# Two graph layers on one core: w of pairs 2 to 27 turned by VectorE and DRAM, filter taps in two row groups, conv results written pair by pair

## The chip, the core and the metric

The kernel runs on 1 core of one Trainium2 chip, in float32 throughout. The metric is the device time of one execution in microseconds (us). PE is TensorE, DVE VectorE, ACT ScalarE, POOL GpSimd and SP SyncE, whose queue issues nearly all DMAs.

## What is computed

There are 64 graphs of 256 nodes with 256 channels, x of shape (64, 256, 256), and a 0/1 adjacency of shape (64, 256, 256). Layer 0, then layer 1:

```python
xc = transpose(x)                                   # channels first
h = relu(bn1(conv1x1(xc)))
x_conv = transpose(relu(bn2(conv17(h, pad=8)) + xc))
s = x @ w_se.T + b_se                               # 3 numbers per node
A = exp(-dist(s)) * adj
x_nmp = A @ relu(x @ w_msg.T + b_msg)
gi = concat(x_conv, x_nmp) @ w_ih.T + b_ih          # r, z, n
gh = x @ w_hh.T + b_hh
r = sigmoid(gi_r + gh_r); z = sigmoid(gi_z + gh_z)
n = tanh(gi_n + r * gh_n)
x = layernorm(x + (1 - z) * n + z * x)
h = layernorm(x)                                    # layer 1
conv = (adj @ h) @ W_rel + b_rel + h @ W_root
x = layernorm(x + x + relu(conv))
```

## The kernel before, in words

**Pairs and blocks.** Graphs go in 32 pairs (`pair(p)`), and the 17-tap convolution in 8 blocks of 8 graphs, four pairs each (`conv1(b)`, then `conv(b)`). The convolution is done by splitting the signal: DVE folds a block (L771) and splits it in a tree of additions and multiplications (L593 to L612 and L679), PE multiplies each leaf by its filter matrix (`product`, L707, tiles ps_k), DVE takes the products out of PSUM (L725 and L726; in block 0 L745) and merges them (L623 to L647), and the last steps (L901 to L905) give the result in slots V0 of X. `kept` (L911) then scales it by the second batch norm and writes it to XC, in slices over the time index j that cover all 8 graphs.

**Filters.** `filters()` makes the leaf matrices once. The 17 taps of 7 output channels are laid side by side by POOL (L542, tile ws), turned by PE (L548, tile tT; ACT evicts, L550), and multiplied by the tap matrix (119 rows, 329 columns; L565, tile ps_w; ACT evicts into W2, L568). There are 74 such blocks of 7 channels, four to a round. The matrices stay in W2 for block 0, and `store_w2` writes them to DRAM; later blocks load them back three at a time into cs (L700).

**One pair.** From xT (x with channels on the partitions) PE makes messages (ps_msg, L1092), distances (ps_sT, ps_dist), and with exp and the mask AT; then ps_nmp (L1139). xc is the conv result plus xT, relu'd (L1145, L1146). The gates (L1179) multiply three sources, xT, nmp and xc, by the gate weights WB: pairs 0, 1 and 31 (`PLAIN`) in 8 plain products (tiles ps_g), the others in 14 products after Strassen's scheme (ps_a, ps_b, ps_d). The tail of the gates (L1246 to L1255) leaves w, which is four times the value to be normed, in wT with channels on the partitions. `norm` turns it back: 8 PE transposes per pair into ps_wT (L1276); ACT copies them to x1 and sums each row (L1285), squares (L1291), and POOL makes the mean and the power -1/2 in q (L1289 to L1300). `project` multiplies wT by both layer-1 matrices (ps_hy, L1311), and DVE scales by q into HY (L1313). `aggregate` multiplies by the adjacency (ps_agg, L1325), adds, norms once more, and stores (L1355). HY, x1 and wT exist once, so a pair waits for the one before to be done with them. Pairs 28 to 31 (`late`) take their statistics on DVE from ps_wT.

**x.** `conv1(b)` fetches x for two graphs (L799 from block 3 on: 16 DMAs of 32 KB in runs of 128 B, so that one DVE operation in 32x32 blocks, L813, finishes the transpose), multiplies (L847), writes relu'd results to DRAM (hd), from where `conv` loads them (L861).

**Order.** Nothing runs as written. Each operation is recorded with a key (`prog.at`, `spread`), and `scheduled` orders each engine's queue by simulated durations and keys; pair p's key is `due = FIRST_GATES + p * PERIOD`, and its steps lie at set distances from it. The order is then fixed: an engine, SP among them, waits at its next instruction. PSUM has 8 banks, with shares: gates 4, conv 3, the rest 6.

Of the kernel before, what the change touches and what calls it, by code (L numbers as in the profile page):

```python
# [54 lines left out]
OB = 7  # L55
HQ = 2 * M * C * (M + 1)
XC_SLOTS = BG + 2
FIRST_GATES, PERIOD, GATE_TIME = 143.0, 60.5, 17.0
AHEAD_FROM, AHEAD_TO, W_DEEP = -20.0, 10.0, 2
CONV1_FROM, CONV1_TO, CONV_FROM, CONV_OUT, CONV_TO = -10.0, 120.0, -6.0, -70.0, -30.0  # L60
PAIR_LEAD, FILTER_LEAD, LOAD_AHEAD = 20.0, 15.0, 12.0
SMALL_RUNS, TURN_FROM = 2.5, 3
# [192 lines left out]
def dram_cells(ap):  # L255

    name = ap.tensor.name
    if not name.startswith(("w2m", "xt", "hd")):
        return []
    dims = list(ap.ap)  # L260
    top = ap.offset + sum(s * (n - 1) for s, n in dims)
    return [(name, u) for u in range(ap.offset // DRAM_UNIT, top // DRAM_UNIT + 1)]


class Engine:
# [4 lines left out]
    def __getattr__(self, method):  # L270
        program, name = self.program, self.name

        def call(*args, hold=(), need=(), lines_up=0, **named):
            line = sys._getframe(1 + lines_up).f_lineno
            outs = [v for v in (named.get("out"), named.get("accum_out"), named.get("out_")) if v is not None]
            outs += [] if "out" in named else [args[0]]
            ins = [v for v in list(args) + list(named.values()) if not any(v is o for o in outs)]
            if method == "matmul" and not named.get("start", True):
                ins.append(outs[0])

            def places(vs):
                return [v if isinstance(v, View) else dram_cells(v) for v in vs
                        if isinstance(v, View) or hasattr(v, "tensor")]
            n = max((v.size() for v in outs if isinstance(v, View)), default=0)
            moved = 0
            if method == "dma_start":
                v = outs[0] if isinstance(outs[0], View) else named["in_"]
                dur, moved = 0.06, v.size() * v.at.shape[0] * 4
                if program.joined is not None:
                    moved *= SMALL_RUNS  # L290
            elif name == "tensor":
                turned = method == "transpose" or named.get("is_transpose")
                dur = 0.109 if turned else 2 * max(0.109, n * 0.8333e-3 + 0.0025)
            elif name == "vector":
                dur = 0.182 if method == "bn_aggr" else 0.147 + 1.044e-3 * (args[1].size() if method == "bn_stats" else n)
                dur += 0.06 * (method == "scalar_tensor_tensor" and isinstance(args[2], View))
            elif name == "scalar":
                dur = 0.16 + 0.83e-3 * n + 0.11 * sum(isinstance(named.get(k), View) for k in ("bias", "scale"))
                dur += 0.2 * ("accum_out" in named)
                where = outs[0].at[0].ravel()  # L300
                dur += 0.9e-3 * n * (n > 1 and "accum_out" not in named and where[1] - where[0] > 1)
            else:
                dur = 1.5 if ALU.pow in args else 0.45 + 1.5e-3 * n
            program.add(name, method, args, named, line, places(ins) + list(need), places(outs) + list(hold), dur, moved)
        return call
# [104 lines left out]
def gnn_two_layers(  # L410
# [66 lines left out]
    xt_dram = tc.dram_tile([B // 2, P, C, 2 * N], F32, name="xt")  # L477
    W2 = sb("w2all", [P, C, NM, D], "first")
    taps = sb("taps", [TAPS * OB, NM * OB], "filters")

# [3 lines left out]
    tb = np.einsum("kf,op->kofp", tap_matrix(), np.eye(OB, dtype=np.float32)).reshape(TAPS * OB, NM * OB)  # L484
# [30 lines left out]
    def filters():  # L515
        pieces, groups = [], []
        for c in range(C):
            for o0, o1 in ((0, 12 * OB), (12 * OB, 24 * OB), (24 * OB, D)):
                starts = [min(o, D - OB) for o in range(o0, o1, OB)]
                for a in range(0, len(starts), 4):  # L520
                    groups.append((len(pieces), starts[a:a + 4]))
                pieces.append((c, o0, o1))
        WT, TT = {}, {}
        WS, AHEAD = {}, 4
        wts = ring("wt", [P, TAPS, D - 24 * OB], 2, "filters")
        wss = ring("ws", [P, 4, TAPS, OB], AHEAD, "filters")
        tTs = ring("tT", [TAPS * OB, 4, P], 2, "filters")
# [8 lines left out]
        def laid(i):  # L536
            piece, starts = groups[i]
            n, o = len(starts), starts[0] - pieces[piece][1]
            if i == 0 or groups[i - 1][0] != piece:
                fetch(piece + 1)  # L540
            WS[i] = next(wss)
            G.tensor_copy(WS[i][:, :n], WT[piece][:, :, o:o + n * OB].rearrange("p k (b o) -> p b k o", o=OB))  # L542

        def turned(i):
            ps, n = bank("ps_tT"), len(groups[i][1])
            with prog.group():
                for k in range(n):
                    PE.transpose(ps[:TAPS * OB, k * P:(k + 1) * P], WS[i][:, k].rearrange("p k o -> p (k o)"), ident)  # L548
            tT = next(tTs)
            A.copy(tT[:, :n].rearrange("k b p -> k (b p)"), ps[:TAPS * OB, :n * P])  # L550
            return tT
# [5 lines left out]
        for i, (piece, starts) in enumerate(groups):  # L557
            c = pieces[piece][0]
            if i + AHEAD < len(groups):
                laid(i + AHEAD)  # L560
            if i + 1 < len(groups):
                TT[i + 1] = turned(i + 1)
            for a, o in enumerate(starts):
                ps = bank("ps_w")
                PE.matmul(ps[:, :NM * OB], TT[i][:, a, :], taps, start=True, stop=True)  # L565
                skip = OB - D % OB if o == D - OB else 0
                pv = ps[:, :NM * OB].rearrange("p (f o) -> p f o", o=OB)
                A.copy(W2[:, c, :, o + skip:o + OB], pv[:, :, skip:])  # L568

# [203 lines left out]
    def graphs_of(b):  # L773
        left, g = BG, 0
        while left:
            slot = (b * BG + g) % XC_SLOTS
            n = min(left, XC_SLOTS - slot)
            yield g, n, slot
            g, left = g + n, left - n

# [3 lines left out]
    def conv1(b):  # L784
# [5 lines left out]
        def fetch(g):  # L790
            if b >= TURN_FROM:
                XN[g] = xn_ahead[:, :4 * D]
                blocks = XN[g].rearrange("p (c g b i) -> p g c b i", c=C, g=2, i=SQ)
                with prog.group():
                    for a in range(P // SQ):
                        for k in range(2):
                            for c in range(C):
                                at = c * P + a * SQ
                                SP.dma_start(out=blocks[a * SQ:(a + 1) * SQ, k, c], in_=x[b * BG + g + k][  # L799
                                    :, at:at + SQ].rearrange("(b j) i -> j b i", j=SQ))  # L800
# [57 lines left out]
    def conv(b):  # L858
# [48 lines left out]
        def kept(js):  # L907
            for o in range(C):
                v = X[:, V0:V0 + M].rearrange("p j (c e) -> p j c e", c=C)[:, js, o, :]
                for g, n, slot in graphs_of(b):  # L910
                    A.activation(XC[:, o, slot:slot + n].rearrange("p g (t j) -> p j g t", j=M)[:, js],  # L911
                                 v[:, :, g * M:(g + n) * M].rearrange("p j (g t) -> p j g t", t=M), AF.Identity,
                                 bias=bn_shift[1][:, o:o + 1], scale=bn_scale[1][:, o:o + 1])

        if b == 0:
            for q in range(4):
                second(q)
                third(q)
                third(q + 4)
                kept(slice(q, M, 4))  # L920
            return
        for j in range(4):
            second(j)
        yield "out"
        for j in range(4):
            third(j)
            third(j + 4)
            kept(slice(j, M, 4))
# [12 lines left out]
    spread(at2, at3, 12.0, 70.0)  # L941
# [47 lines left out]
    prog.at(58.0, 0.01)  # L989
# [8 lines left out]
    nmp = nmps[:, 1:5].rearrange("p (c g) n -> p c g n", c=C)  # L998

# [17 lines left out]
    run(first)  # L1017
    at6 = len(prog.ops)
    spread(at4, at6, 33.0, FIRST_GATES - 4)
    conv1(1)  # L1020
# [20 lines left out]
    for c in range(C):  # L1041
        V.tensor_scalar(beta[:, c, :], ones, gb[:, 1, c:c + 1], None, ALU.mult)
# [26 lines left out]
    def pair(p):  # L1069
# [98 lines left out]

        def product(ps, i, second, start):
# [33 lines left out]
        if plain:  # L1203
            prog.at(due, 2 * GATE_TIME / 44)
            for gs in ((0,), (1,)) if apart else ((0, 1),):
                for T in (RG, ZN):
                    for f in range(C):
                        for g in gs:
                            a = bank("ps_g", "gate")
                            for k in range(C):  # L1210
                                product(a, (f, k, g), T is ZN, k == 0)
# [52 lines left out]
        def norm(gs):  # L1264
# [5 lines left out]
            for g in gs:  # L1270
# [34 lines left out]
        def project(gs, q):  # L1305
            prog.at(due + 2 * GATE_TIME + 8, 0.6)
# [8 lines left out]
        def aggregate(gs):  # L1315
            prog.at(due + 2 * GATE_TIME + 16, 0.4)
# [47 lines left out]
    for b in range(NB):  # L1364
# [11 lines left out]
        if b + 1 < NB:  # L1376
# [6 lines left out]
            run(coming)  # L1383
            at3 = len(prog.ops)
            spread(at1, at2, start + CONV_FROM, start + span + CONV_OUT)
            spread(at2, at3, start + span + CONV_OUT, start + span + CONV_TO)
            if b + 2 < NB:
# [85 lines left out]
```

## Time and profile before

| | |
|---|---|
| Median of 3 runs (lowest, highest) | 2065.92 us (2064.77, 2066.36) |
| The profiled execution, its span | 2065.45 us, 2063.7 us |
| Mean granted PE clock | 0.995 |
| Busy: PE, DVE, ACT, POOL | 2029.6, 1678.4, 1047.5, 296.9 us |
| PE idle: hrow waiting for L1042; nmp for L1132; ps_wT for L1255 | 6.3, 6.2, 3.4 us |
| DMA | 241.21 MB in 284683 packets, 110469 of them under 512 B |
| L1276 on PE, L813 on DVE, L799 on SP | x256 (busy 33.7 us), x20 (1239 ns), x320 (median 449 ns) |
| PE: L548 and L565; ACT: L550 and L568 | 10.9 and 43.7 us; 11.0 and 33.2 us |

The span runs from the first to the last instruction; the execution's own time is 1.75 us longer. A group line has the line of the code, the engine, the operation, out<-in, shapes and count, then busy time and the mean of one in ns. Matmul durations overlap[...]. A window line has the stretch, its length, busy time (and instructions) of PE, weight loads, DVE, ACT and POOL, the granted clock, the mean busy share of 16 DMA engines, and GB/s. A timeline line has start, duration, engine, line, operation, tiles and count; brackets hold idle time ahead of it and what ended it.

### The profile page before, as it was taken

Reading aid. Unit: us, or ns where it says so; the run is one execution under the profiler, and the core shown is the slowest. Engines: PE = TensorE matmul, PEld = TensorE weight load, DVE = VectorE, ACT = ScalarE, POOL = GpSimd, SP = SyncE. Lnnn points to the kernel's source line nnn. Section 1 sums busy time; section 2 is a strip of 40 time slices with the busy share of each in tenths; the row PEclk is TensorE's granted clock in tenths of the full one; section 3 lists DMA queues with packets and bytes.
Section 4 is the critical chain, followed back from the end, with each engine's and each line's share of the span. In section 5 each row is a group of like instructions: output and inputs, shape, how many; then the busy total and the mean of one; then the engine's idle time right before and its main releaser. Section 6 shows DMA issues by size and latency. Waiting matters only on the chain.

```text
span 2063.7 us, 28744 instructions
## 1 busy us (share of the span) xinstructions
PE 2029.6 (98%) x10332; PEld 1645.4 (80%) x10332; DVE 1678.4 (81%) x2587; ACT 1047.5 (51%) x2460; POOL 296.9 (14%) x520
## 2 busy tenths in 40 slices
PE   9989999999999999999999999999999999999997
PEld 6868779778887788877887778877888778887875
DVE  7983798899968998889968998799887899875644
ACT  7453534754446544565447544475445554465432
POOL 4010210111111111101101121112110111111100
PEclk9999999999999999999999999999999999999999
DMA  8834363334433264334532354333452224211100
GB/s 213 265 99 156 105 205 121 105 120 146 152 97 113 78 184 138 95 100 125 176 98 97 101 155 149 104 116 84 151 159 80 72 77 153 93 38 61 41 21 31
DMA packets 284683, 241.21 MB, mean 117 GB/s; under 512 B 110469, under 2 KB 269180, under 8 KB 284540
## 3 DMA queue, kind: packets, MB, share of 16 engines
q1 hardware_dynamic: 283998, 238.94, 37.8%
q8 instruction: 82, 1.34, 0.3%
q14 instruction: 61, 0.50, 0.1%
q10 hardware_dynamic: 542, 0.43, 0.1%
HBM read 177.85 MB, written 61.47 MB: 116 GB/s over the span
## 4 chain that ended last, share of the span: by engine, by line
PE 92%; DVE 5%; ACT 1%; issue 1%; POOL 0%; POOLq 0%; DVEq 0%; ACTq 0%
PE ps_a L1179 21%; PE ps_k L707 15%; PE ps_hy L1311 10%; PE ps_d L1179 10%; PE ps_msg L1092 5%; PE ps_agg L1325 5%; PE ps_b L1179 5%; PE ps_nmp L1139 5%; PE ps_c L847 5%; PE ps_g L1179 4%; PE ps_w L565 2%; PE ps_wT L1276 1%; DVE XF L679 1%; PE ps_dist L1125 1%; PE ps_tT L548 0%
## 5 line engine op out<-in xcount | busy, mean ns | idle before, releaser
L707 PEld LDWEIGHTS ps_k<-XF,cs 128*128 128x128 f32 x2632 | 316.3, 192 | 15.6 <-issue 9.6
L707 PE MATMUL ps_k<-XF,cs 128*128 128x128 f32 x2632 | 318.3, 275 | 0.0
L1311 PE MATMUL ps_hy<-wrr,wT 128*128 128x512 f32 x512 | 228.3, 593 | 1.5 <-ACT XF L724 1.5
L1179 PE MATMUL ps_a<-nmp,WB 128*128 128x256 f32 x696 | 207.5, 380 | 0.0
L1311 PEld LDWEIGHTS ps_hy<-wrr,wT 128*128 128x128 f32 x512 | 95.4, 190 | 103.0 <-issue 92.1
L1191 ACT COPY ZN<-ps_a 128x512 f32<-128x512 f32 x116 | 68.0, 586 | 194.1 <-PE ps_a L1179 193.8
L1179 PE MATMUL ps_a<-tx,WB 128*128 128x256 f32 x522 | 158.2, 385 | 0.2
L1193 ACT ACTIVATE RG<-ps_a,bhh 128x512 f32<-128x512 f32 x116 | 79.2, 683 | 139.9 <-PE ps_a L1179 107.2
L1179 PEld LDWEIGHTS ps_a<-nmp,WB 128*128 128x128 f32 x696 | 132.5, 190 | 18.3 <-ACT nmp L1141 0.2
L1335 ACT ACTIVATE HY<-HY 128x256 f32<-128x256 f32 x112 | 45.7, 408 | 177.9 <-DVE HY L1329 172.4
L1092 PE MATMUL ps_msg<-wms,xT 128*128 128x260 f32 x512 | 133.4, 383 | 0.0
L679 DVE TENSOR_TENSOR XF<-XF 128x512 f32<-128x512 f32 (+3 forms) x128 | 126.3, 1009 | 5.3 <-ACT XF L760 3.3
L1139 PE MATMUL ps_nmp<-AT,msg 128*128 128x256 f32 x512 | 120.6, 384 | 6.4 <-DVE AT L1132 6.2
L1313 DVE SCALAR_TENSOR_TENSOR HY<-ps_hy,q,hrow 128x512 f32<-128x512 f32 x128 | 95.4, 747 | 36.1 <-PE ps_hy L1311 31.8
L1325 PE MATMUL ps_agg<-HY,adja 128*128 128x256 f32 x512 | 120.1, 380 | 2.6 <-DVE HY L1313 2.6
L1325 PEld LDWEIGHTS ps_agg<-HY,adja 128*128 128x128 f32 x512 | 96.1, 190 | 29.5 <-issue 12.9
L1139 PEld LDWEIGHTS ps_nmp<-AT,msg 128*128 128x128 f32 x512 | 96.3, 192 | 21.9 <-DVE AT L1132 6.6
L1179 PEld LDWEIGHTS ps_a<-tx,WB 128*128 128x128 f32 x522 | 94.4, 191 | 21.2 <-issue 6.9
L847 PE MATMUL ps_c<-xTc,w 128*128 128x512 f32 x232 | 107.5, 594 | 1.4 <-ACT xTc L827 1.4
L1092 PEld LDWEIGHTS ps_msg<-wms,xT 128*128 128x128 f32 x512 | 93.4, 190 | 14.2 <-issue 1.8
L1179 PE MATMUL ps_a<-xc,WB 128*128 128x256 f32 x348 | 103.6, 379 | 0.8 <-ACT xc L1146 0.8
L1289 POOL TENSOR_SCALAR total<-total 128x4 f32<-128x4 f32 x28 | 13.5, 484 | 631.4 <-ACT x L1285 631.4
(205 smaller groups left out, 4519.7 us busy)
## 6 DMA issues: line engine op xcount, KB each, us to landing
cs<-w2m SPq DMA_DIRECT2D x105, 768.0 KB, 4.9
adjm<-in_adjT_dram SPq DMA_DIRECT2D x64, 256.0 KB, 2.8
xT<-xt SPq DMA_DIRECT2D x32, 512.0 KB, 3.9
adja<-in_adjT_dram SPq DMA_DIRECT2D x64, 256.0 KB, 2.7
out_dram<-HY SPq DMA_DIRECT2D x64, 256.0 KB, 2.1
hd<-xn SPq DMA_DIRECT2D x28, 544.0 KB, 3.3
XF<-hd SPq DMA_DIRECT2D x28, 544.0 KB, 4.2
xt<-xTc SPq DMA_DIRECT2D x29, 512.0 KB, 2.7
```

Source lines behind the costliest of these rows:

```text
L679: (V.tensor_add if add else V.tensor_sub)(sl(o, n), sl(a, n), sl(b, n))
L707: PE.matmul(ps[:, o * P:(o + 1) * P], w(m, c)[:, o * P:(o + 1) * P], X[:, slot, c * P:(c + 1) * P], start=first and o == 0 and c == 0, sto ...
L847: PE.matmul(ps, w1[:, c, o * P:(o + 1) * P], xTc[:, c, :], start=(c == 0), stop=(c == C - 1), hold=[h[:, :, o]])
L1092: PE.matmul(ps[:, :D + 4], xT[:, c, g, m * P:(m + 1) * P], wms[:, c, :], start=(c == 0), stop=(c == C - 1 and not idle), hold=[msg[:, g, m]])
L1139: PE.matmul(ps[:, d * N:(d + 1) * N], msg[:, g, m, d * P:(d + 1) * P], AT[:, g, m, :], start=(m == 0), stop=(m == C - 1), hold=[nmp[:, :, g]])
L1179: PE.matmul(ps[:, h * N:(h + 1) * N], block[:, s, gate, :], right[s][at], start=start and h == 0 and j == 0, stop=j == len(sources) - 1, s ...
L1191: A.copy(o, ps)
L1193: A.activation(o, ps, AF.Identity, bias=bhh[:, 2, f:f + 1])
L1311: PE.matmul(ps, wT[:, 2 * f + g, m * P:(m + 1) * P], wrr[:, f, :], start=(f == 0), stop=(f == C - 1), hold=[HY[:, g, m]], need=[] if apart ...
L1313: stt(HY[:, g, m, :], ps, q[:, 1, j:j + 1], hrow)
L1325: PE.matmul(ps[:, n_ * D:(n_ + 1) * D], adja[:, g, m, n_ * P:(n_ + 1) * P], HY[:, g, m, :D], start=(m == 0), stop=(m == C - 1))
L1335: A.activation(HY[:, g, m, :D], y[:, m, :], AF.Copy, accum_out=total[:, j:j + 1])
```

## The change

Four things change.

1. For pairs 2 to 27, `norm` no longer uses PE. DVE turns wT in 32x32 blocks into HY's first half, four DMAs write the blocks to a DRAM tile in runs of 128 B, such that whole rows come to stand there, and four DMAs read them into x1. ACT copies and sums from x1, the copies going to HY. `project` and `aggregate` of these pairs get keys 17.4 later.
2. Filters are made in rounds of two row groups: a block has 3 output channels (51 rows), one transpose turns two blocks (at rows 0 and 64), and their products go to two PSUM banks, three blocks side by side in each; one ACT copy evicts 3 blocks (423 elements). The tap matrix stands twice in the 128 rows. POOL lays each half by itself, and zeroes the tiles once. The planner's price of a PE product with 51 rows is multiplied by 0.52 and with 4 rows by 0.36.
3. `conv` runs all of the last steps first and then writes xc pair by pair (`kept(q)`), each at its own key 8 apart; in pairs 0 and 1, the gates' products with xT and nmp are recorded ahead of those with xc. The small product of beta moves from DVE to ACT.
4. x is fetched by 8 DMAs of 64 KB instead of 16, and keys and constants change.

```diff
-OB = 7
+OB, OG = 3, 64
-FIRST_GATES, PERIOD, GATE_TIME = 143.0, 60.5, 17.0
+FIRST_GATES, PERIOD, GATE_TIME = 126, 59.2, 17.0
-CONV1_FROM, CONV1_TO, CONV_FROM, CONV_OUT, CONV_TO = -10.0, 120.0, -6.0, -70.0, -30.0
-PAIR_LEAD, FILTER_LEAD, LOAD_AHEAD = 20.0, 15.0, 12.0
-SMALL_RUNS, TURN_FROM = 2.5, 3
+CONV1_FROM, CONV1_TO, CONV_FROM, CONV_OUT, CONV_TO = -10.0, 120.0, -6.0, -58.0, -30.0
+PAIR_LEAD, FILTER_LEAD, LOAD_AHEAD = 20.0, 15.0, 16.4
+SMALL_RUNS, TURN_FROM = 1.3, 3
+FILTERS_TO, STORES_AT = 50.0, 55.0
+KEEP = 8.0
+W_FROM, W_LAG = 2, 17.4
...
+                if not turned:
+                    dur *= {51: 0.52, 4: 0.36}.get(args[1].at.shape[0], 1.0)
...
+    w_dram = tc.dram_tile([2, SQ, 2 * C * C, P // SQ, P], F32, name="wd")
-    taps = sb("taps", [TAPS * OB, NM * OB], "filters")
+    taps = sb("taps", [P, NM * OB], "filters")
...
-            G.tensor_copy(WS[i][:, :n], WT[piece][:, :, o:o + n * OB].rearrange("p k (b o) -> p b k o", o=OB))
+            for g in range(2):
+                at = o + g * n * OB
+                G.tensor_copy(WS[i][:, :n, g, :TAPS * OB].rearrange("p b (k o) -> p b k o", o=OB),
+                              WT[piece][:, :, at:at + n * OB].rearrange("p k (b o) -> p b k o", o=OB))
...
-                    PE.transpose(ps[:TAPS * OB, k * P:(k + 1) * P], WS[i][:, k].rearrange("p k o -> p (k o)"), ident)
+                    PE.transpose(ps[:, k * P:(k + 1) * P], WS[i][:, k].rearrange("p g e -> p (g e)"), ident)
...
-            for a, o in enumerate(starts):
-                ps = bank("ps_w")
-                PE.matmul(ps[:, :NM * OB], TT[i][:, a, :], taps, start=True, stop=True)
...
-                A.copy(W2[:, c, :, o + skip:o + OB], pv[:, :, skip:])
+            pss, size = [bank("ps_w") for _ in range(2)], NM * OB
+            with prog.group():
+                for k in range(n):
+                    for g in range(2):
+                        r = slice(g * OG, g * OG + TAPS * OB)
+                        PE.matmul(pss[g][:, k * size:(k + 1) * size], TT[i][r, k, :], taps[r, :], start=k == 0,
+                                  stop=k == n - 1, skip_group_check=True)
+            for g in range(2):
...
+                pv = pss[g][:, :n * size].rearrange("p (b f o) -> p f b o", b=n, o=OB)
+                to = W2[:, c, :, first:done].rearrange("p f (b o) -> p f b o", o=OB)
+                A.copy(to[:, :, :, skip:], pv[:, :, :, skip:])
...
-                        for k in range(2):
-                            for c in range(C):
-                                at = c * P + a * SQ
-                                SP.dma_start(out=blocks[a * SQ:(a + 1) * SQ, k, c], in_=x[b * BG + g + k][
-                                    :, at:at + SQ].rearrange("(b j) i -> j b i", j=SQ))
+                        for c in range(C):
+                            at = c * P + a * SQ
+                            SP.dma_start(out=blocks[a * SQ:(a + 1) * SQ, c], in_=rows_of[:, :, at:at + SQ])
...
-        def kept(js):
+        def kept(q):
+            slot = (b * BG + 2 * q) % XC_SLOTS
             for o in range(C):
...
+                at = o * P + 2 * q * M
+                A.activation(XC[:, o, slot:slot + 2].rearrange("p g (t j) -> p j g t", j=M),
+                             X[:, V0:V0 + M, at:at + 2 * M].rearrange("p j (g t) -> p j g t", t=M), AF.Identity,
+                             bias=bn_shift[1][:, o:o + 1], scale=bn_scale[1][:, o:o + 1])
...
-        for j in range(4):
+        for j in range(8):
             third(j)
-            third(j + 4)
-            kept(slice(j, M, 4))
+        for q in range(BG // 2):
+            yield q
+            kept(q)
...
+    def keep(steps, key):
+        for q in range(BG // 2):
+            prog.at(key + KEEP * q)
+            next(steps, None)
...
+    keep(first, FIRST_GATES - 20)
...
-        V.tensor_scalar(beta[:, c, :], ones, gb[:, 1, c:c + 1], None, ALU.mult)
+        A.activation(beta[:, c, :], ones, AF.Identity, scale=gb[:, 1, c:c + 1])
...
-                            for k in range(C):
-                                product(a, (f, k, g), T is ZN, k == 0)
+                            for ks in ((0, 1), (2,)) if not apart else ((0, 1, 2),):
+                                products_of(a, f, g, T is ZN, ks)
...
-            for g in gs:
+            if not late and p >= W_FROM:
+                blocks, placed = HY[:, 0].rearrange("p m e -> p (m e)"), w_dram[p % 2]
+                V.transpose(blocks.rearrange("p (k c n) -> p k c n", c=C, n=P),
+                            wT.rearrange("p (c g) (m n) -> p (g m) c n", c=C, m=C))
+                with prog.group():
+                    for a in range(P // SQ):
+                        SP.dma_start(out=placed.rearrange("j k b e -> j (k b) e")[:, :, a * SQ:(a + 1) * SQ],
+                                     in_=blocks[a * SQ:(a + 1) * SQ].rearrange("j (k i) -> j k i", i=SQ))
+                with prog.group():
+                    for b in range(P // SQ):
+                        SP.dma_start(out=x1[b * SQ:(b + 1) * SQ].rearrange("j g m (c e) -> j (g m c) e", e=P),
+                                     in_=placed[:, :, b, :])
+                for g, m, j in spots(gs):
+                    source[j] = x1[:, g, m, :]
+                    A.activation(HY[:, g, m, :D], x1[:, g, m, :], AF.Copy, accum_out=total[:, j:j + 1])
+            for g in gs if late or p < W_FROM else ():
                 ps = bank("ps_wT")
...
-            prog.at(due + 2 * GATE_TIME + 8, 0.6)
+            prog.at(due + 2 * GATE_TIME + 8 + (0.0 if late or p < W_FROM else W_LAG), 0.6)
...
-            prog.at(due + 2 * GATE_TIME + 16, 0.4)
+            prog.at(due + 2 * GATE_TIME + 16 + (0.0 if late or p < W_FROM else W_LAG), 0.4)
...
+            keep(coming, start + span + CONV_TO)
```

`products_of(ps, f, g, second, ks)` is new: it issues, for both halves of a gate bank, the products of only those sources (0 xT, 1 nmp, 2 xc) that are in `ks`, over both halves of the channels.

## The prediction

> **What bounds the kernel now.** I read engine shares and chain of waits first, then the groups by form, the windows, and timelines of three places.
>
> ```profile
> PE 2029.6 (98%) x10332; PEld 1645.4 (80%) x10332; DVE 1678.4 (81%) x2587; ACT 1047.5 (51%) x2460; POOL 296.9 (14%) x520
> PE 92%; DVE 5%; ACT 1%; issue 1%; POOL 0%; POOLq 0%; DVEq 0%; ACTq 0%
> ```
>
> TensorE (PE) is busy 98% of the span and is 92% of the chain: in the steady part, PE work taken away is time taken away. Its length per pass (a matmul instruction; a float32 product is two) I read from start to start, not from the durations, which overlap:
>
> ```profile
> 1017.81 1.04 PE L1276 MATMUL ps_wT<-ident,wT 128*128 128x128 f32 x8
> 1018.68 5.52 PE L707 MATMUL ps_k<-XF,cs 128*128 128x128 f32 x48
> 1027.53 7.03 PE L1311 MATMUL ps_hy<-wrr,wT 128*128 128x512 f32 x16
> 1034.39 3.62 PE L1325 MATMUL ps_agg<-HY,adja 128*128 128x256 f32 x16
> ```
>
> Eight transposes take 0.87 us (0.109 each), a pass of 512 columns 0.429, of 256 0.216. So columns pass at 1.2 per ns[...].
>
> The first 152 us are another stage, without pair gates:
>
> ```profile
> 28.90 2.38 PE L565 MATMUL ps_w<-taps,tT 119*128 119x329 f32 x8
> 31.11 0.60 PE L548 MATMUL ps_tT<-ident,ws 128*119 128x128 f32 x4
> 71.82 23.60 PE L707 MATMUL ps_k<-XF,w2all 128*128 128x128 f32 x208
> 152.06 1.06 PE L1179 MATMUL ps_g<-xT,WB 128*128 128x256 f32 x2
> ```
>
> PE makes filters until 71.82 without a gap. VectorE's (DVE's) timeline beside it:
>
> ```profile
> 27.75 1.21 DVE L597 SCALAR_TENSOR_TENSOR XF<-XF 128x1024 f32<-128x1024 f32 x1
> 77.02 2.16 DVE L679 TENSOR_TENSOR XF<-XF 128x1024 f32<-128x1024 f32 x3
> 79.24 0.69 DVE L745 TENSOR_TENSOR XF<-XF,ps_k 128x512 f32<-128x512 f32 x1
> ```
>
> From 24.9 to 79.24 DVE folds and splits the first block's signal, also without a gap, and only then takes the first product out of PSUM, waiting for nobody. PE's head start from 71.82 to 79.24 filled the conv's three banks. So two chains arrive here together, and shortening PE's alone moves nothing behind 79.24.
>
> ```profile
> 130.00:140.00 10.00, 7.17 (x26) 3.62 (x25) 9.76 (x16) 7.58 (x15) 2.75 (x7) 1.00 0.92 287
> 140.00:150.00 10.00, 5.36 (x14) 1.97 (x14) 7.49 (x14) 6.43 (x8) 0.00 (x0) 0.66 0.40 138
> 150.00:160.00 10.00, 9.66 (x38) 7.46 (x38) 9.11 (x13) 4.94 (x9) 0.32 (x2) 0.83 0.07 28
> ```
>
> At 137 to 152 PE idles while DVE ends the first conv, then starts the gates at a granted clock of 0.66 to 0.83.
>
> [...] eight 256-column passes of L1125 take 0.64 us (114.09 to 114.73), 0.08 each instead of 0.216. [...] (three POOL copies, and DVE operations that take 0.68 alone):
>
> ```profile
> 47.45 3.18 POOL L542 COPY ws<-wt 128x476 f32<-128x476 f32 x3 [1.92 <-PE ps_tT L548]
> 48.12 1.00 DVE L612 SCALAR_TENSOR_TENSOR XF<-XF 128x512 f32<-128x512 f32 x1
> 49.04 1.11 DVE L610 SCALAR_TENSOR_TENSOR XF<-XF 128x512 f32<-128x512 f32 x1
> ```
>
> [...] No store in 128 B runs is in this trace; loads in 128 B runs are (L799).
>
> **Step 1: w turned off PE (pairs 2 to 27).** Removed: 26 x 8 = 208 transposes of 0.109 us = 22.7 us of PE, all in the PE-bound part. Added on DVE: 26 of the operation of L813, 1.24 us, 32 us in all. DVE is at most 184 of 200 us busy there (600 to 800), so 4 us more per 200 fits; uncovered it would be those 32 us. ScalarE (ACT) reads x1 from SBUF instead of PSUM, 408 against 387 ns, x104: 2 us, nothing at 51%. SP issues eight more DMAs per pair, 208 of 0.45 us, and 160 fewer x loads (8 instead of 16 per fetch); each readback waits on SP for the landed write, with loads of cs, x and adj queued behind it.
>
> The new length is the round trip through DRAM. Write: 4 DMAs, 4,096 runs of 128 B. Lower bound: in the window 848 to 850 the L799 loads used 0.28 of 16 engines at 43 GB/s, which is 13.3 ns per run, so 3.4 us over 16 engines, and 1.8 to land: 5.2. Upper: a whole L799 fetch of 4,096 runs takes 8.9 us to issue (842.57 to 851.5), and 1.8: 10.7. Read: a 512 KB load (L808) lands in 3.9; doubled for half-size runs 7.8. Together 9.1 to 18.5 us; I take 13, since the write is spread over four issues only.
>
> Is it covered? In the pair at 1000, the gates end at 1007.5, wT is ready at 1015.5 (8.0), and from the first copy of L1285 to q is 8.1 us (1018.48 to 1026.54). New: 8.0 + 1.24 + round trip + 8.1 after the gates' end. Adding pass lengths in the changed kernel's PE order gives the distance from each pair's last gate to its first ps_hy: 26.8 to 52.6 us for these 26 pairs (19 to 22 before), five under 29. The ps_agg that must have HY comes 6.9 us later, and needs q 1.5 earlier (two HY results of 0.75), so the allowed round trip is distance - 11.9: at least 14.9 us. At 13, no pair stalls; at 18.5 eight do, 15 us in sum; at 20 ten, 29 us. DVE also waits for the earlier pair's store of HY, about 22 us after that pair's ps_hy. For such queueing I put **+2 us**.
>
> **Step 2: filters in two row groups.** PE before: 74 x (0.109 + 2 x 0.277) = 49 us. After: 86 transposes (9.4) and 172 matmuls of two 141-column passes of 0.12 us, 41.3 one by one, 20.6 at two side by side: 30. So 19 us less PE; if the groups don't overlap, 2 more. But ACT still evicts all: a copy grows 1.0 ns per element (329: 459 ns, 188: 316), so 423 take 0.55, 56 of them 31 us, and with the tT copies (0.48 x 28) and remainders 46 us, against 44 before. At 1.59 us per round from 25 on, ACT ends near 70. POOL makes 60 small copies instead of 20. The small ones took 0.51 to 0.65, back to back under DVE 1.06; 52 copies from 20 us on, at 0.85 to 1.06, with the 3.5 us of half_z and half_r, end at 64 to 78. Any end before 76 is hidden, since PE needs only 3.5 us before DVE's first take at 79.24. **The 19 us become PE idle ahead of that take: worth nothing.** [...] 14 copies stretched DVE by 4.1 us (0.3 each; what its operations of 27 to 66 us took above their shape's usual time); 52 copies at 0.3 would cost 11.5 more, at equal cost per element nothing. I take +5; and +1.7 for the clock after PE's idle.
>
> **Step 3: order at the first gates.** In the changed order PE's non-filter work ahead of pair 0's first xc product is larger by the x and nmp products of four gate banks, 24 matmuls x 2 x 0.216 = 10.4 us, and smaller by L1054's sums (1.7): 8.7 us done while DVE still works. These products then run warm; before, they lost some 1.9 us at the cold clock. When does xc come? Before: the last L905 ends at 143.34, gates at 152.06, 8.7 us. After: four copies of 128x512 (L911, 1.26 us) and the relu (1.05) ahead of it, 6.3: -2.4. The last fold comes 0.7 earlier (six transposes fewer ahead of it). L1042 on ACT frees the hrow product of DVE's queue (6.3 us idle), which only lets PE reach the same wait. Shift of that point: -0.7 - 2.4 + 5 + 1.7 = +3.6. Gain: 8.7 + 1.9 - 3.6 = **7.0 us**.
>
> Writing xc pair by pair is 64 copies of 1.26 = 81 us of ACT, 88 before; nothing. The next block's folds wait for the last of them; DVE's slack covers that.
>
> **Sum.** The profiled execution took 2065.45 (span 2063.7). 2065.45 - 22.7 - 7.0 + 2 = 2037.8, and the median shown lies 0.5 higher: **2038 us**. By itself this case spans 2026 to 2050 (shift of xc 0 to +12, stalls 0 to 10).
>
> **Rivals.**
> (a) *The round trip outlasts its cover.* ps_hy and HY's products wait on DVE for q, and ps_agg on them. For it: 128 B stores are unmeasured and SP is in order. Against: 41% mean DMA share in 400 to 600. It eats the gain from a trip of 20 us (29 us lost); at 22 it loses 53: about 2091, slower. 6%.
> (b) *The filters become late:* POOL at 1.06 a copy reaches 78 and DVE loses 11.5: xc 12 to 15 us later than forecast, 2051. 14%.
> (c) *The first stage gives more than I allow:* DVE loses nothing to POOL, no stalls, the take moves with the fold: -5 - 1.7 - 2, 2029; if PE's 19 us counted in full, 2065.9 - 22.7 - 19 = 2024. 18%.
> (d) *The row groups don't overlap:* PE's filters end near 72 as now, hidden by DVE; the time stays 2038.
> Forecast 62%, with (d) inside.
>
> **Chances.** About 0.2% (4 us) can be told from no change, so the limits are 2061.8 and 2070. Slower: (a), 0.06. Same: the tail of (b) with a few long trips, 0.04. Faster 0.90. The range 2022 to 2056 takes in (c) and most of (b).
>
> **What would show it.** Right: eight ps_wT passes gone per pair, PE still over 97% busy after 200; PE idle between the filters' end (68 to 76) and DVE's first take (80 to 88); four gate banks opened before xc, xc products near 153 to 158; w's landing 10 to 15 us after its transpose. Wrong: PE waits at L1325 or L1311's successors with q late by more than 5 us (a); a first take after 88 (b) or before 79 (c).

## The result, and the profile after

| | before | after |
|---|---|---|
| Median (lowest, highest) | 2065.92 us (2064.77, 2066.36) | 2054.09 us (2050.28, 2059.44) |
| Profiled execution, span | 2065.45, 2063.7 us | 2055.2, 2053.4 us |
| Mean granted PE clock | 0.995 | 0.985 |

The ratio is 0.9951 (95% interval 0.994 to 0.9963): faster by 11.8 us, where 27.9 were forecast. Against the forecast's sum for the profiled execution, 2037.8, 17.4 us are missing; the rest of this document looks for them.

The page of the kernel after, engine shares and chain of waits:

```profile
PE 2010.2 (98%) x10332; PEld 1632.0 (79%) x10332; DVE 1703.5 (83%) x2611; ACT 1033.2 (50%) x2418; POOL 310.4 (15%) x564
PE 91%; DVE 6%; ACT 1%; DMA 1%; issue 1%; POOL 1%; SPq 0%; POOLq 0%; ACTq 0%; DVEq 0%
```

PE still bounds, but its busy time fell by 19.4 us where the forecast had taken out 22.7 for w and 19 for the filters; work done at half clock counts in it at almost twice its length (below, 1.78 us instead of 0.99 for the products of one round). What PE waits for is another list than before (line waited for: us in total, times, longest):

```profile
PE ps_k L731 <- DVE XF L703: 7.1, 1, 7.1
PE ps_a L1209 <- ACT RG L1223: 6.7, 6, 2.8
PE ps_agg L1370 <- issue: 6.5, 1, 6.5
PE ps_tT L562 <- POOL ws L555: 6.1, 5, 2.7
```

None of the four stands in the list of before in this way (there ps_agg waited 2.6 us, in two pieces). The first, third and fourth belong to single places: the next block's first product (at 267), the last pair, and the filters. The second is six short waits of gate products between 478 and 1846.

**The first stage.** The DVE timeline of after, at the splits' end and the first take of a product (L769, before L745):

```profile
76.61 2.19 DVE L703 TENSOR_TENSOR XF<-XF 128x1024 f32<-128x1024 f32 x3
93.28 0.69 DVE L769 TENSOR_TENSOR XF<-XF,ps_k 128x512 f32<-128x512 f32 x1 [14.48 <-PE ps_k L731]
```

DVE ends its splits at 78.8 (79.2 before); POOL cost it nothing that shows there. Then it waits 14.48 us for PE. The windows of after (PE, weight loads, DVE, ACT, POOL, granted clock, DMA share, GB/s):

```profile
30.00:40.00 10.00, 7.29 (x53) 5.87 (x55) 9.83 (x10) 4.57 (x12) 9.74 (x11) 0.67 0.75 185
40.00:50.00 10.00, 9.52 (x80) 8.10 (x78) 9.83 (x17) 7.63 (x19) 7.58 (x12) 0.65 0.24 54
50.00:60.00 10.00, 7.36 (x77) 5.58 (x77) 9.86 (x7) 7.66 (x20) 10.00 (x8) 1.00 0.13 30
60.00:70.00 10.00, 9.46 (x58) 7.44 (x60) 9.62 (x16) 4.67 (x10) 9.13 (x15) 0.54 0.90 278
70.00:80.00 10.00, 10.00 (x61) 7.61 (x59) 8.60 (x14) 5.49 (x12) 4.53 (x7) 0.50 1.05 356
```

PE idles 6.4 us between 30 and 70, POOL is busy for 7.6 to 10.0 of every 10 us, and the granted clock is at half for long. In windows of 0.2 us from 30 to 47 and from 57 to 83 the clock reads 1.00 or 0.50, but for the windows in which it changes. Read as such a mix, the windows above and the next (0.94) hold (0.33 + 0.35 + 0.46 + 0.50 + 0.06) x 20 = 34 us of half clock. The PE timeline of after shows how it goes:

```profile
55.11 0.99 PE L584 MATMUL ps_w<-taps,tT 51*128 51x141 f32 x12
56.03 0.55 PE L562 MATMUL ps_tT<-ident,ws 128*128 128x128 f32 x3
56.51 0.99 PE L584 MATMUL ps_w<-taps,tT 51*128 51x141 f32 x12
60.24 0.55 PE L562 MATMUL ps_tT<-ident,ws 128*128 128x128 f32 x3 [2.74 <-POOL ws L555]
60.72 1.78 PE L584 MATMUL ps_w<-taps,tT 51*128 51x141 f32 x12
...
75.51 0.90 PE L562 MATMUL ps_tT<-ident,ws 128*128 128x128 f32 x3
76.34 1.78 PE L584 MATMUL ps_w<-taps,tT 51*128 51x141 f32 x12
78.06 1.54 PE L562 MATMUL ps_tT<-ident,ws 128*128 128x128 f32 x6
79.53 1.78 PE L584 MATMUL ps_w<-taps,tT 51*128 51x141 f32 x12
81.24 0.55 PE L562 MATMUL ps_tT<-ident,ws 128*128 128x128 f32 x3
...
85.59 1.67 PE L731 MATMUL ps_k<-XF,w2all 128*128 128x128 f32 x11
```

PE waits 2.74 us for POOL, and 0.5 us after it has begun again the same products take 1.78 instead of 0.99. The rounds then follow with only one more wait, of 0.30 us, yet the clock is back only at 81.2. At half clock a round takes 2.55 us (75.51 to 78.06). The row groups do overlap: from 55.11 to 56.03 there are twelve passes in 0.92 us, 0.077 each. The forecast had 0.06, which was its author's estimate (0.12 halved): the trace of before has row groups side by side in L1125, four of 4 rows (0.08 us per pass of 256 columns instead of 0.216).

**The trip of w.** One pair's timeline in after (the turn, four writes, four reads, ACT's first use):

```profile
1020.00 1.25 DVE L1302 STREAM_TRANSPOSE HY<-wT 128x1024 f32<-128x1024 f32 x1
1021.28 3.68 SPq L1306 DMA_DIRECT2D wd<-HY  x4
1028.26 2.54 SPq L1310 DMA_DIRECT2D x<-wd  x4
1040.04 0.41 ACT L1314 ACTIVATE HY<-x 128x256 f32<-128x256 f32 x1
```

The turn ends at 1021.25 and the last read is issued by 1030.80. In this pair it landed at 1037.07, 6.9 us after its issue began, which makes a trip of 15.8 us. Over the 26 pairs, from the turn's end to the last landing on record, the trip took 9.7 to 19.6 us, the median 13.1; 13 was forecast. First ps_hy comes 18.7 to 33.3 us after the turn, and no PE wait in the list goes back to q or x1. But the gate waits (ps_a for ACT, 6.7 us) stand in after and not in the run without the turn below; ahead of the longest, at 1667, ACT had waited 4.98 us for DVE's wT.

### The profile page after: what moved, and what is told of

Same layout as the page of the kernel before. It is cut to its first block, busy times and chain, and to the rows that moved or that the text cites. A ratio compares the mean times of both kernels' runs of the same rounds, so it can differ in the third digit from the quotient of the medians.

```text
span 2053.4 us, 28839 instructions
## 1 busy us (share of the span) xinstructions
PE 2010.2 (98%) x10332; PEld 1632.0 (79%) x10332; DVE 1703.5 (83%) x2611; ACT 1033.2 (50%) x2418; POOL 310.4 (15%) x564
## 4 chain that ended last, share of the span: by engine, by line
PE 91%; DVE 6%; ACT 1%; DMA 1%; issue 1%; POOL 1%; SPq 0%; POOLq 0%; ACTq 0%; DVEq 0%
PE ps_a L1209 20%; PE ps_k L731 16%; PE ps_hy L1356 11%; PE ps_d L1209 10%; PE ps_agg L1370 5%; PE ps_msg L1110 5%; PE ps_nmp L1157 5%; PE ps_b L1209 5%; PE ps_c L862 5%; PE ps_g L1195 4%; PE ps_w L584 1%; PE ps_dist L1143 1%; POOL ws L555 1%; DVE XF L636 1%; DVE XF L634 1%
## 5 line engine op out<-in xcount | busy, mean ns | idle before, releaser
L1110 PEld LDWEIGHTS ps_msg<-wms,xT 128*128 128x128 f32 x512 | 95.1, 190 | 13.8 <-issue 1.3
L1209 PE MATMUL ps_d<-nmp,WB 128*128 128x256 f32 x348 | 103.5, 379 | 0.0
```

The costliest lines, as they stand in the source:

```text
L1110: PE.matmul(ps[:, :D + 4], xT[:, c, g, m * P:(m + 1) * P], wms[:, c, :], start=(c == 0), stop=(c == C - 1 and not idle), hold=[msg[:, g, m]])
L1209: PE.matmul(ps[:, h * N:(h + 1) * N], block[:, s, gate, :], right[s][at], start=start and h == 0 and j == 0, stop=j == len(sources) - 1, s ...
```

## The experiments

Theory A: the filters end late, because POOL feeds PE too slowly and PE then runs at a low clock. Theory B: the round trip, or the order of the work, ate the gain. Each run was timed against the kernel before on its own chip; 0.01 of ratio is 20.7 us.

### Filters of before

```diff
-OB, OG = 3, 64
+OB = 7            # and filters(), taps as before: 20 copies, 119 rows, one group
```

> The changed kernel with the filters of the kernel before (blocks of 7, 119 rows, one group, 20 copies on POOL), all else as changed. Theory A (the filters end late because POOL's 60 small copies feed PE too slowly, and PE then works at a low clock): DVE's first take of a product goes from 93.3 back to 79 to 81 us, the first xc product of a gate comes 9 to 14 us earlier, and the time is 2040 to 2046. Theory B (the loss lies in the round trip of w or in the order, and the filters are hidden as forecast): within 4 us of the changed kernel, 2050 to 2058.

Measured: 2041.62 us, ratio 0.9887 (0.9872 to 0.9901), 13 us better than after. First take at 80.01, clock 1.00 in every window from 20 to 100. The filters' new form cost what is gained by undoing it, which is theory A's case.

### One copy per round

```diff
-            for g in range(2):
-                at = o + g * n * OB
-                G.tensor_copy(WS[i][:, :n, g, :TAPS * OB]..., WT[piece][:, :, at:at + n * OB]...)
+            G.tensor_copy(WS[i].rearrange("p b g e -> p (b g) e")[:, :2 * n, :TAPS * OB]...,
+                          WT[piece][:, :, o:o + 2 * n * OB]...)
-            ps, n = bank("ps_tT"), rounds[i][2]
+            ps, n = bank("ps_tT", "conv"), rounds[i][2]
```

> The changed kernel with one POOL copy per round of filters in place of two (30 copies of 306 elements instead of 60 of 153; the two row groups take alternate blocks of three filters, so that block and group are one dimension); PE's and ACT's work is the same. Theory A with POOL as the cause: PE no longer waits for POOL's copies, the filters end before 76, the first take is at 79 to 81, and the time 2040 to 2046. If ACT's evictions or PE's clock are the cause and not POOL: the first take stays after 88 and the time above 2050.

The second part of the edit, ps_tT's share of the PSUM banks, belongs to it and to the next run; that share alone was not changed in any run.

Measured: 2045.24 us, ratio 0.9903 (0.9888 to 0.9918), 10 us better than after. Its windows:

```profile
30.00:40.00 10.00, 10.00 (x110) 7.85 (x111) 9.83 (x10) 10.00 (x23) 9.50 (x11) 1.00 0.82 177
40.00:50.00 10.00, 9.67 (x108) 7.52 (x106) 9.90 (x13) 9.46 (x23) 9.37 (x11) 1.00 0.43 99
50.00:60.00 10.00, 10.00 (x109) 7.85 (x108) 9.83 (x10) 10.00 (x23) 5.98 (x5) 1.00 1.08 367
```

These are the same products, with ACT now full, POOL done before 60, and a full clock. PE starts ps_k at 64.32 (85.59 in after), and DVE, which has no wait, takes at

```profile
80.32 0.68 DVE L766 TENSOR_TENSOR XF<-XF,ps_k 128x512 f32<-128x512 f32 x1
```

So from 64 to 80 PE's lead is hidden, as forecast. The first xc product comes 14.9 us earlier than in after (149.29 against 164.21), but only 10 us reach the end: PE then waits elsewhere (the 7.1 us at the next block stay, and 4.9 us of idleness come in 200 to 250).

### Eight buffers

```diff
-        WS, AHEAD = {}, 4
+        WS, AHEAD = {}, 8    # and the bank's share for ps_tT as in the run above
```

> The changed kernel with eight buffers instead of four between POOL's copies and PE's transposes (the same 60 copies), so that POOL runs ahead during the first conv. If short gaps of PE while it waits for POOL start the half clock, and POOL's own pace of about 0.86 us a copy would do: fewer gaps, half clock for less than the 32 us of the changed kernel, filters end at 74 to 80, time 2042 to 2048. If POOL's pace alone decides: filters end at 80 or later, 2050 to 2055.

Measured: 2044.84 us, ratio 0.9919 (0.9889 to 0.9948). All 60 copies are there, 16 of them done before 20.3, and the first gap is gone. Its PE timeline:

```profile
60.21 0.55 PE L562 MATMUL ps_tT<-ident,ws 128*128 128x128 f32 x3 [3.22 <-POOL ws L555]
60.68 1.76 PE L584 MATMUL ps_w<-taps,tT 51*128 51x141 f32 x12
...
67.84 1.54 PE L562 MATMUL ps_tT<-ident,ws 128*128 128x128 f32 x6
69.31 1.78 PE L584 MATMUL ps_w<-taps,tT 51*128 51x141 f32 x12
71.03 0.55 PE L562 MATMUL ps_tT<-ident,ws 128*128 128x128 f32 x3
...
75.39 2.78 PE L731 MATMUL ps_k<-XF,w2all 128*128 128x128 f32 x21
```

There is one long gap, 10.2 us of half clock (60.7 to 71.0), and the filters end at 75.4, inside the forecast's 64 to 78. So with the same 60 copies they can end 10 us earlier than in after: what after adds lies in how closely POOL and PE are tied together, by buffers or by banks. Three of the four executions took 2043.9 to 2045.4 us at a mean clock of 0.991, one took 2057.12 at 0.982.

### Filler matmuls

```diff
             with prog.group():
+                for _ in range(2):
+                    PE.matmul(pss[0][:, 3 * size:], ones, ones[:, :512 - 3 * size], start=True, stop=True, ...)
                 for k in range(n):
```

> The changed kernel with two idle 89-column matmuls (0.44 us at full clock, result unread) ahead of each round of filter products, POOL's 60 copies untouched. If the low granted clock, not POOL's pace itself, is what makes the filters late: PE's clock stays at 0.9 or more from 30 to 80 us, a round takes 1.9 us to its end, the filters end at 78 to 81, and the time is 2046 to 2050. If POOL's pace alone counts: filters end at 84 or later, time 2054 or more.

Measured: 2077.89 us, ratio 1.0071 (1.0056 to 1.0086). The first expectation failed, since the clock was not kept; the figures of the second came true, but not for its reason, since POOL was no longer full. Three of its windows:

```profile
30.00:40.00 10.00, 7.93 (x50) 6.65 (x48) 9.79 (x11) 3.51 (x8) 9.74 (x12) 0.70 0.55 131
50.00:60.00 10.00, 10.00 (x61) 8.71 (x57) 9.86 (x8) 4.11 (x9) 6.58 (x5) 0.50 0.34 79
90.00:100.00 10.00, 10.00 (x81) 8.96 (x81) 0.00 (x0) 4.98 (x12) 1.58 (x6) 0.73 0.01 1
```

After one wait of 2.00 us for POOL, until 33.1, the clock is at half for 61 us with PE busy all the time. So here 61 us of work without gaps did not win the clock back. The filters end at 107.4; how late the clock alone makes them this run can't say, since the filler itself takes 0.92 to 1.08 us of each round at half clock.

### One gap, in either form of the filters

Three runs repeat a single POOL copy so that PE waits once. The repeats write the same data.

```diff
-            G.tensor_copy(WS[i]..., WT[piece]...)
+            for _ in range(14 if i == 6 else 1):      # 19 in the second run; 16 if i == 8 in the third
+                G.tensor_copy(WS[i]..., WT[piece]...)
```

> The changed kernel with the filters of before (119 rows, one group) and 13 repeats of one POOL copy early in them, so that PE waits some 3 to 6 us once. It is there for the granted clock after that gap. If any steady stream of matmuls wins the full clock back: half clock for 4 to 6 us. If a filter stage keeps a full clock but does not win it back, as the two-row-group rounds of the changed kernel: half clock for over 10 us.

> The changed kernel with the filters of before (119 rows, one row group) and 18 repeats of one POOL copy, so that PE waits some 4 to 6 us once in the filters; it is there for the granted clock after the gap. If the 119-row stream wins the clock back like the conv and gate products (half for 6 to 8 us after a gap of 6 us): half clock for at most 10 us. If filter rounds of any form don't: longer than 10 us.

> The changed kernel with one POOL copy per round (two row groups of 51 rows) and 15 repeats of one copy, so that PE waits some 4 to 6 us once in the filters. If rounds in two row groups of 51 rows keep a full clock but don't win it back: half clock for 15 us or more, as in the changed kernel, and the filters end after 80. If it was POOL's repeated gaps that held the clock down there: half clock for at most 8 us, and the filters end by 74.

The first made PE wait for only 1.7 us, in two pieces, and the clock stayed at 1.00; on its question it is inconclusive (2038.01 us, one execution). In the second PE waited 8.7 us and began again at 48.60:

```profile
48.00:52.00 4.00, 2.67 (x7) 1.93 (x8) 3.93 (x6) 0.58 (x1) 4.00 (x5) 0.50 0.00 0
52.00:56.00 4.00, 4.00 (x16) 2.97 (x15) 3.96 (x8) 2.28 (x5) 0.85 (x2) 0.62 0.79 183
56.00:60.00 4.00, 4.00 (x17) 2.77 (x17) 3.86 (x7) 3.49 (x9) 3.60 (x6) 1.00 0.30 62
```

The full clock was back 6.4 us after the restart, with one more wait of 0.73 us in between (2053.7 us, one execution). In the third, with two row groups of 51 rows, PE waited 12.3 us and began again at 47.26:

```profile
48.00:52.00 4.00, 4.00 (x25) 3.02 (x26) 3.97 (x8) 2.23 (x5) 3.35 (x6) 0.50 0.64 155
...
64.00:68.00 4.00, 4.00 (x23) 2.88 (x22) 3.93 (x4) 2.05 (x7) 3.93 (x4) 0.50 0.21 37
68.00:72.00 4.00, 3.72 (x33) 3.01 (x31) 3.83 (x9) 2.54 (x7) 1.47 (x3) 0.74 1.14 330
```

The half clock lasted for 22.8 us of gapless work (2063.72 us, one execution), and the filters ended by 88 (ACT is full until there, and busy for 0.06 of the next 2 us). The gaps of the second and third run were longer than meant. In each of them one gap sufficed (8.7 and 12.3 us). That the form of the rounds decides how long the half clock lasts is likely but not shown: there is one case with 119 rows, and in rounds of 51 rows the clock came back between 10.8 us after the restart (eight buffers) and 22.8 us.

The clock records show a pattern that goes further. The stretches at half clock in the filters last whole numbers of intervals of 3.41 us: 4 and 6 in after (13.65 and 20.48 us), 3 with eight buffers (10.2), 18 with the filler (61.4). Where a timeline shows rounds of 51 rows winning the full clock back, the six transposes of two rounds ran one after the other in the last interval: at 45.36 and 78.06 in after, 67.84 with eight buffers, 67.57 in the third run here, and 77.38 in the run without the turn below. In none of these timelines did an interval without such a run of six bring it back. Six at 47.26 in the third run here (PE had just begun again) and at 55.58 (across the border of two intervals) did not. These are observations; which property of the rounds matters was not tried, and stays open.

### Without the turn of w

```diff
-W_FROM, W_LAG = 2, 17.4
+W_FROM, W_LAG = 32, 0.0
```

> The changed kernel with w of pairs 2 to 27 turned on PE again (208 transposes back), filters and conv results as changed. Theory A (the turn is worth its 22.7 us of PE, less 2 of queueing): 2073 to 2079, slower than before the change. Theory B (the round trip makes PE wait and eats half of it): 2060 to 2066.

Measured: 2077.23 us, ratio 1.006 (1.0043 to 1.0077), 0.0109 above after: 22.5 us, where 22.7 less 2 were forecast. The two intervals leave some 4 us either way, and the two profiled executions differ by 16.8 us only. From 400 to 1900 PE idles 8.8 us in after and 3.5 in this run, so the turn seems to cost some 5 us of waits, not half of its gain: theory B's case did not come.

### The turn alone, and with one helper or both

```diff
 kernel before, with the turn, W_LAG, PERIOD 59.2, LOAD_AHEAD 16.4, SMALL_RUNS 1.3; then
+x fetched in 8 DMAs                    # second and fourth run
+xc written pair by pair, CONV_OUT -58  # third and fourth run
```

> The kernel before with only the turn of w for pairs 2 to 27 moved to DVE and DRAM (with the lag and the period of the planner that go with it), filters and conv results as before. Theory A: 2043 to 2047, nearly the whole 22.7 us. Theory B: 2052 to 2058, as the full change.

> The kernel before with the turn of w moved (as in the run of the turn alone, which took 2109 us) and, besides, the x fetches in 8 DMAs instead of 16. If the turn alone is slow because SP's queue is full of x DMAs and its waits for w's landing: the waits of the conv for cs go (11 us there), and the time falls to 2060 to 2085. If it is slow because the conv results come late for another reason (the wait of 21.9 us of ps_a on xc): it stays above 2095.

> The kernel before with the turn of w moved and, besides, the conv results written pair by pair (x fetches in 16 DMAs, filters and gate products as before). If the gates wait because xc of all four pairs is written in four quarters: the 21.9 us of ps_a on xc go, and the time falls to 2070 to 2088. If SP's queue is the cause: it stays above 2095.

> The kernel before with the turn of w moved, conv results written pair by pair and the x fetches in 8 DMAs; filters, gate products and beta as before. If the turn needs both helpers and the order at the first gates brings nothing of its own: 2040 to 2044, as the changed kernel with the filters of before (2041.6). If the order at the first gates is worth the 7 us of the forecast: 2046 to 2051.

| | time | ratio (interval) | PE idle 400 to 1900 | mean clock |
|---|---|---|---|---|
| before | 2065.92 us | 1 | 9.7 us | 0.995 |
| turn alone | 2109.46 | 1.022 (1.0202 to 1.0237) | 54.6 | 0.985 |
| with x in 8 DMAs | 2067.14 | 1.0015 (1.0008 to 1.0022) | 25.2 | 0.988 |
| with xc by pairs | 2061.88 | 0.9994 (0.9987 to 1.0002) | 22.0 | 0.993 |
| with both | 2049.66 | 0.9929 (0.9914 to 0.9944) | 16.5 | 0.993 |

Both theories missed the first: the turn alone makes the kernel slower by 45 us. With one helper the time can hardly be told from that of before. Two PE waits of the turn alone:

```profile
PE ps_a L1181 <- ACT xc L1148: 21.9, 5, 6.3
PE ps_k L709 <- DMA cs<-w2m: 11.0, 7, 3.7
```

The x fetches in 8 DMAs take the second away, the pairwise xc the first, as expected of each; the time with xc by pairs fell below its forecast (2070 to 2088), and that with both lies in its second case. Each brings more than its wait (42 and 47 us), and both together bring 60, less than the sum. Of the turn alone's 41.6 us more span, 44.9 are idleness in the steady part and 22.7 less are work. The remaining 19 fit the lower mean clock (an estimate from the table: 0.010 of 2105 us, 21 us), so that PE's busy time fell by 2.5 us only. Which gap comes from which queue was not taken apart further. The planner's constants came with all four runs; neither they nor a helper were tried without the turn, so part of these figures may be theirs.

### What was left, mended

```diff
 one copy per round, and:
-AHEAD_FROM, AHEAD_TO, W_DEEP = -20.0, 10.0, 2
+AHEAD_FROM, AHEAD_TO, W_DEEP = -40.0, -10.0, 2
 last pair, first graph: keys of the gates' tail, norm, project and aggregate
+ - 24.0
```

> The changed kernel with one POOL copy per round (as in the run of 2045.2 us), the next block's first conv put 20 us earlier in the planner's order, and the last pair's first graph let past the second graph's last gates. If the remaining loss is the 7.1 us wait for the next block's split signal and some 4 us of the tail: 2033 to 2037. If other waits take their place: 2041 or more.

> The changed kernel with the filters of before, the next block's first conv put 20 us earlier in the planner's order and the last pair's first graph let past the second's last gates (as in the run of 2034.7 us, which has row groups with one copy per round). If the filters are hidden behind DVE in both: within 4 us of that run, 2030 to 2038. If two row groups with one copy bring PE time after all: 2040 or more.

Measured: 2034.73 us, ratio 0.9861 (0.9847 to 0.9876), and with the filters of before 2036.62 us, 0.9864 (0.9848 to 0.9881). By their ratios both beat the change by 18 us. The two lines of the first one's PE waits that answer to after's first and third:

```profile
PE ps_agg L1368 <- DVE HY L1356: 4.8, 1, 4.8
PE ps_k L728 <- DVE XF L700: 0.6, 1, 0.6
```

Of the 7.1 us 0.6 are left, and 6.5 became 4.8. Against the run with one copy alone the gain is 0.0042, 8.7 us; with the filters of before the same edits bring 0.0023, 4.8 us, so with intervals of 3 us either way the gain is only roughly known. The two forms of filters end within each other's intervals: the row groups as such are worth nothing that these runs can tell, as step 2 said.

## Why the prediction was right and wrong

**Step 1, the turn: right in size, wrong in its conditions.** The gain was 22.5 us by the medians and 16.8 by the profiles, against 22.7 less 2; the trip took 13.1 us against 13, in two pairs 19.3 and 19.6, with no wait of PE for q; rival (a) did not come. But the step priced the x fetches as "160 fewer x loads" on the side, and step 3 the pairwise xc at "nothing". They are worth 42 to 60 us to it: without them the turn loses 45 us, with one of them it gains nothing. The profile of before had a hint, SP's 8.9 us per x fetch with cs queued behind; the sum priced SP's new DMAs by their number and not by what stands behind them.

**Step 2, the filters: here the forecast failed.** The step that failed is "52 copies from 20 us on, at 0.85 to 1.06 ... end at 64 to 78. Any end before 76 is hidden", with "+1.7 for the clock after PE's idle". Measured: filters end at 85.6, first take 93.28 instead of 79.24. POOL's pace was right (18.41 us for 20 copies, 0.92 each), and with eight buffers the filters ended at 75.4, inside the bound (its own terms add up to 68 to 79, not 64 to 78). Wrong was that POOL was laid beside PE as a separate chain. With four buffers they are one: POOL waited 13.8 us for PE, PE 6.1 us for POOL, and after its waits of 2.00 and 2.74 us PE was at half clock, for 34 us in all, which costs up to 17 us of PE work where 1.7 were allowed. From 60 on rounds at half clock (2.55 us) are the bound, not POOL (1.84 for a round's two copies). PE's round is also 1.40 us, not 1.07 (0.48 for three transposes, 0.92 for twelve passes). Against that, DVE lost none of the 5 us allowed for POOL's copies (splits ended at 78.8, before at 79.2). Nor did the head start fill "the conv's three banks": with one copy PE worked on conv products from 64.32 to 89.81 without a wait, and DVE's first take came at 80.32. The outcome is that of rival (b), given 14%, in its size (2051 forecast, 2054 measured), but it came by the clock: (b) had POOL reach 78 and DVE lose 11.5. In time the filters cost 13 us by the run with the filters of before, 10 by the run with one copy.

**Step 3, the order at the first gates: gained and given back.** The work moved ahead of xc is real: with both helpers and the old order of the gates the ratio is 0.9929, with the new order 0.9887 (the run with the filters of before), 8.7 us better (7.0 forecast), though other constants differ too. In after the first gates ran at a clock of 1.00 (140 to 160), where before had 0.66 and 0.83. But the step did not say what is late next. With the pass lengths added up in PE's order (an estimate), block 1's fourth conv1 stands at 184 us of PE work, as before (185), while its first product moved from 235 to 217: 33 us between them instead of 50. So PE reaches it 7.1 us before DVE's splits are ready (260.4 to 267.6 idle), and the clock is at half for 4.7 us more. A like thing happens at the end: the last pair's gates of one bank are a single group in the changed order, in the trace the first graph's transposes and projection come only after all of them, and ps_agg waits 6.5 us once, then runs at half clock. The runs with both moved gain 8.7 and 4.8 us; the two places were not moved apart.

**The sum.** From after to one copy it is 10 us, to the mended order 8.7 us more; with the filters of before 13 and 4.8. On the scale of before's 2065.92 us the ratios 0.9861 and 0.9864 are 2037.2 and 2037.8 us, within 1 us of the forecast of 2038. The 17.4 missing us are thus found, in the filters and in the two waits of step 3. The first was named at too small a price, the others not at all. The chance of faster was right, the 62% for the first case too much: nothing in it stood for waits that a shorter PE queue uncovers. That 2054 fell into the range of 2022 to 2056 is luck as far as the clock goes: the range had made room for a slow POOL, not for PE at half clock.

## What to carry to other kernels

When two engines feed each other through a few buffers, don't price them as two chains: ask where the slower one makes the faster one wait, and what that wait does to its clock (here waits of 2.00 and 2.74 us, and 34 us of half clock after them). Where PE work is taken away or moved ahead, measure the distance to the next thing PE waits for; that place can take the gain (here 7.1 us at 267). Here a step that adds DMAs to SP's queue was worth its sum only once the queue's other work had been thinned and the results that PE waits for came earlier (2109.46 us without, 2049.66 with both).

## What the runs showed of the hardware

- In after, waits of 1.58 us (at 1865), 2.00 and 2.74 were followed by half clock, while one of 2.81 us (at 1667) was not, nor 1.7 us in two pieces in the first gap run: in these runs the length of one wait alone does not decide. The half clock lasted 3.41, 6.83, 13.65 and 20.48 us there, whole multiples of 3.41, apart from the stretch that the kernel's end cut off. The conv's products won the full clock back in 4.7 us (267.6 to 272.3 in after), the 119-row filters in 6.4 after the gap that was set. Rounds of 51-row products in two row groups with their transposes needed 10.8 us with eight buffers, 14.6 and 21.0 in after, 22.8 after the one gap that was set, and 62 with small filler matmuls, while with one copy per round they kept it (1.00 from 20 to 64). So in these runs gapless work was not the same as work that wins back the clock.
- In two row groups, passes of 51 rows and 141 columns took 0.077 us each at full clock and 0.143 at half (twelve in 0.92 us, 55.11 to 56.03, and in 1.71 us, 66.17 to 67.88 in after).
- Writes of 128 KB in runs of 128 B landed 3.4 us after issue (median; 2.6 to 7.1) and their reads 3.1 (2.6 to 8.0), at 0.52 mean DMA share in 500 to 1000. The forecast's 7.8 us for the read (3.9 doubled for half-size runs) was its author's estimate; in the pair at 1020 the four reads took 8.8 from the first issue to the last landing. The forecast's 9.1 to 18.5 us for the trip held 24 of the 26 pairs, the other two took 19.3 and 19.6.
